# Batch 0's second half of outputs: transposed, as four units of seven block products, ahead of batch 1's folding

## The chip, the cores and the metric

The kernel runs on one core of a Trainium2 chip. The core has five engines with queues of their own: TensorE (PE, matrix products; PEld is its weight load), VectorE (DVE), ScalarE (ACT), GpSimd (POOL) and SyncE (SP, which here only issues DMAs). ACT and POOL issue DMAs too. Every engine works off its own queue in order and waits there for semaphores. The metric is device time in microseconds; the profile is one execution, taken by the hardware profiler.

## The reference

Two batches of 1024 tokens with 1024 features. After a layer norm, two linear maps are taken of the normed input, one with a block-masked weight and a bias (s), one with a dense weight plus a mixture of eight low-rank updates whose coefficients depend on the batch's mean token (y). The output is `x + s * silu(y)`.

```python
xn = _layernorm(x, axis=-1)
# s: blocks of 32x32 of the weight are dropped where the mask's block sum is 0
s = jnp.einsum('bsk,nk->bsn', xn, w_masked) + bias
# y: E = 8 updates of rank R = 64, mixed by coeffs of each batch
base = jnp.einsum('bsi,oi->bso', xn, W_org)
q = jnp.einsum('bi,ki->bk', xn.mean(axis=1), Wq)
coeffs = jax.nn.softmax(jnp.einsum('bk,ek->be', q, lora_keys) / math.sqrt(K), axis=-1)
h = jnp.einsum('bsi,eir->bser', xn, lora_down)
delta = jnp.einsum('be,bser,ero->bso', coeffs, h, lora_up)
g = _silu(base + delta)
x = x + s * g
```

All data are float32, and each product is made of three products of parts: a value is split into a high part (a copy into the type float32r, by ACT) and a low part (the difference, by DVE), and high x high, high x low and low x high are summed in PSUM. So a product of a 128x128 weight with 128x512 data costs three matmuls, and a contraction of 512 costs twelve, one *group*.

## The kernel before

**Folding.** The mixture is linear in the weights, so for each batch the kernel folds the low-rank part into the dense weight: W = W_org^T + down · (coeff · up). `scale_up` multiplies the 512 rows of `up` by the coefficients of the batch and splits them (four tiles `cut`). One *fold* (`y_prep`, `y_mul`, `y_sum`) makes 128 rows of 512 output columns of W: load a block of `down` (tile `ds`) and one of W_org (tile `wo`), split `ds` into `dhi` (ACT) and `dlo` (DVE), twelve matmuls into a PSUM tile `psw` (two of these), and an add on DVE of `psw` to `wo`. A half of the output (512 columns, `h`) takes eight folds (`kt`), a batch sixteen.

**Batch 0, plainly.** Tokens stand in PSUM's partitions: a `gemm` of one tile of 128 tokens and 512 output columns takes eight rows of the contraction, 24 matmuls. The order on PE is: a ramp with the first half (h = 0) of s; eight folds for y, h = 0 (L826); the phase y, h = 0, eight gemm tiles with the eight folds for h = 1 between them (`jobs_b`); the phase y, h = 1 (`jobs_c`), with the masking of the s weights of h = 1 beside it; then `s_tile`, the gemm tiles of s, h = 1, with batch 1's sixteen folds between them (L1075). The results of the first map of each pair stay in `stash`; `final_evac` multiplies, adds x and leaves the store to ACT (`store_late`).

**Batch 1, transposed, with seven products.** Here outputs stand in the partitions and tokens in the columns. A *unit* is a pair of blocks of 128 outputs for one of the maps (s or y), for all 1024 tokens: a 2x2 block product over halves of the contraction and halves of the tokens, done as seven block products instead of eight (Strassen's scheme in Winograd's form). `quad` (L1157) does a unit: seven groups of twelve matmuls, 84, into three PSUM tiles (`pa`, `pb`, `py`), with copies and adds between (`snap`, L1178, L1192, L1202, L1203). The seven sums of the data side are made once: `wide_load`, `wide_norm` (L911) and `wide_b` norm batch 1's transposed input and form differences, POOL stores them to DRAM (`xv`, `store_sums`), and `fill` loads and splits them into the tiles `xw`. The weight side is made for each unit one quad ahead: `unit_load` (s from the input `wu`, y from the folded weights `yu`, which the folds stored to DRAM from ACT), `unit_mask`, `unit_sum`, `unit_split`. There are eight units, and units 2k and 2k+1 share their outputs: the first writes `gate` tiles, the second multiplies, and `out_tile` adds x by a DMA that accumulates onto the SBUF tile (L1130, issued by POOL), after which SP stores the tile (L1134). The last unit loads x ahead instead (`res_load`).

**Means.** Batch 1's means and variances come from DVE (`bn_stats`, `nat_stats` L164), 16 instructions of 128x512.

**What sets the order.** On PE, DVE, ACT and POOL the program's own order holds (`manual_schedule`, L617); SP's order is chosen at build. Tiles come from pools with a fixed number of buffers; a tile that takes over a buffer waits until its last user is done, a DMA included. The pool `stage` has one tag `st` of six buffers of 128x512 which `ds`, `wo`, `us` and others share.

Of the kernel before, what the change touches and what calls it, by code (L numbers as in the profile page):

```python
# [32 lines left out]
def kernel(  # L33
# [25 lines left out]

    nc = tc.nc  # L60
# [31 lines left out]
    ones_r = c0pool.tile([P, P], F32R, name="ones_r")  # L92
    nc.vector.memset(ones_r.bitcast(F32), 1.0)
# [21 lines left out]
    keys_sb = c0pool.tile([P, E_], F32, name="keys_sb")  # L115
# [30 lines left out]
    def rstd_of(t):  # L146

        mv = small.tile([P, 2], F32, name="mv", bufs=10)
        nc.vector.bn_aggr(mv, stat[t])
        ve = small.tile([P, 1], F32, name="ve", bufs=3)  # L150
        nc.vector.tensor_scalar(ve, mv[:, 1:2], EPS, None, ALU.add)
        nc.gpsimd.tensor_tensor(rstd[:, t : t + 1], ve, mhalf, ALU.pow)
        means[t] = mv[:, 0:1]
# [10 lines left out]
    def nat_stats(b, i):  # L164
        t = b * TPB + i
        xn = nat_tile()
        nc.sync.dma_start(xn, x[t * P : (t + 1) * P, :])
        bn(t, xn, 0)
        bn(t, xn, 1)
        rstd_of(t)  # L170
# [87 lines left out]
    def mask_part(qr, c):  # L258
        mt = nat_tile(I32)
# [10 lines left out]
    def s_mul(dst, h, kt):  # L270
        st = stage.tile([P, NH], F32, name="ws", tag="st", bufs=6)
        nc.sync.dma_start(st, wT[kt * P : (kt + 1) * P, h * NH : (h + 1) * NH])
        v = st.rearrange("p (b i) -> p b i", i=32)
        nc.vector.tensor_tensor(
            v, v, m_sb[:, kt, 16 * h : 16 * (h + 1)].unsqueeze(2).to_broadcast([P, 16, 32]), ALU.mult
        )
        nc.scalar.copy(dst[:, kt, 0, :], st)  # L277
        staged[("s", h, kt)] = st

    def s_lo(dst, h, kt):  # L280
        st = staged.pop(("s", h, kt))
        nc.vector.tensor_tensor(dst[:, kt, 1, :], st, dst[:, kt, 0, :].bitcast(F32), ALU.subtract)


    csel = {}

    def coeffs(b):


        def sums():  # L290
# [3 lines left out]
            for h in range(2):  # L294
                ps = ps_s.tile([P, 4, P], F32, name="xrow", tag="ps_s")
# [14 lines left out]
        def query():  # L310
            qh = small.tile([P, 2], F32, name="qh")
            for h in range(2):
# [5 lines left out]
                else:  # L318
                    mp = csel[b][h]
                junk = stage_l.tile([P, NH], F32, name="junk", tag="g", bufs=2)  # L320
                nc.vector.scalar_tensor_tensor(
                    junk, mp, 1.0, wq_sb[:, h * NH : (h + 1) * NH], ALU.mult, ALU.mult, accum_out=qh[:, h : h + 1]
# [7 lines left out]
        def scores():  # L330
            sp = ps_s.tile([P, E_], F32, name="sp", tag="ps_s")
# [27 lines left out]
    def scale_up(b, h, homes=()):  # L359
        cu[(b, h)] = []  # L360
        for c in range(4):
            t = cupool.tile([P, 2, NH], F32R, name="cut", tag="cu")
            st = homes[c] if c < len(homes) else stage.tile([P, NH], F32, name="us", tag="st", bufs=6)
            nc.sync.dma_start(st, up[c * P : (c + 1) * P, h * NH : (h + 1) * NH])
# [8 lines left out]
    def y_prep(b, h, kt):  # L373
        ds = stage.tile([P, 4, P], F32, name="ds", tag="st", bufs=6)
        nc.sync.dma_start(ds, down[kt])
        ws = stage.tile([P, NH], F32, name="wo", tag="st", bufs=6)
        nc.sync.dma_start(ws, worgT[kt * P : (kt + 1) * P, h * NH : (h + 1) * NH])
        dhi = stage.tile([P, 4, P], F32R, name="dhi", bufs=2)
        dlo = stage.tile([P, 4, P], F32R, name="dlo", bufs=2)
# [21 lines left out]
    def y_add(dst, b, h, kt):  # L401
        y_sum(b, h, kt)
        y_hi(dst, b, h, kt)

# [4 lines left out]
    def y_fin(dst, b, h, kt):  # L409
        y_add(dst, b, h, kt)  # L410
        y_lo(dst, b, h, kt)
# [52 lines left out]
    def final_evac(kind, b, h, i, ps, res):  # L464
        t = b * TPB + i
        mine = stage_l.tile([P, NH], F32, name="mine", tag="g", bufs=2)
        if kind == "s":
            s_evac(mine, ps, b, i, h * NH, NH)
        else:
            y_evac(mine, ps, b, i)  # L470
        nc.vector.tensor_tensor(mine, mine, stash[(b, h, i)], ALU.mult)
# [815 lines left out]
```

## Time and profile before

| | us |
|---|---|
| three runs | 458.43, 462.94, 462.17; median 462.17 |
| the profiled execution | 462.08 |
| its span, first to last instruction | 460.1 |
| PE busy | 444.7 |
| DVE busy | 305.1 |
| ACT busy | 169.3 |
| POOL busy | 59.5 |
| bytes moved by DMA | 89.52 MB, 195 GB/s on average |

Stages by PE's work, in us from the start of the span: ramp and s, h = 0, of batch 0 to 70.6; folds for y, h = 0, to 92; the phase y, h = 0, with folds to about 160; the phase y, h = 1, to about 212; s, h = 1, with batch 1's folds to 305.7; eight quads, the last matmul ending at 455.2; the last adds and stores to the end.

A line of a group reads: line, engine, operation, tile written from tiles read, shapes, number of instructions | busy us, mean ns of one | idle time of the engine before them and what ended it. In a windows row the busy time and number of instructions of each engine follow the stretch's length, then the clock granted to PE (1.00 is full), the mean busy share of the 16 DMA engines, and GB/s. In a list of DMAs the last number is the median time from issue to landing. In a list of waits the three numbers are the total, the number of waits and the longest.

### The profile page before, as it was taken

The numbers are of one execution on the slowest core, as the hardware profiler recorded it, in microseconds if no ns is written. First come the engines' busy times: TensorE is split into PE (matmuls) and PEld (weight loads), VectorE is DVE, ScalarE is ACT, GpSimd is POOL, SyncE is SP. The second block draws the span as 40 slices with busy tenths as digits, with TensorE's granted clock in tenths as the row PEclk, the third lists the DMA queues.
The fourth block names the chain that finished last, engine by engine and source line by source line (L and its number), as shares of the span: only waits on it lengthen the run. The fifth ranks groups of instructions, "written<-read, shape, count | busy, mean of one in ns | idle before, by whom it ended". The sixth has DMA issues, their size and how long they took to land.

```text
span 460.1 us, 5752 instructions
## 1 busy us (share of the span) xinstructions
PE 444.7 (97%) x2047; PEld 365.4 (79%) x2047; DVE 305.1 (66%) x492; ACT 169.3 (37%) x277; POOL 59.5 (13%) x72
## 2 busy tenths in 40 slices
PE   7799999999999999997999999999999999999995
PEld 5689888888887888885888788877888888888884
DVE  5889778666775788866546776669466294465624
ACT  3576624363323132213324233158243422441510
POOL 3764210000010202230000000000020020002000
PEclk9899999999999999997999999999999999999999
DMA  8995406687862586799778985664274246218003
GB/s 267 390 350 196 146 24 205 183 281 255 287 230 93 186 317 227 277 309 303 243 249 276 297 274 152 207 219 137 79 147 134 85 98 177 91 24 220 31 1 114
DMA packets 47404, 89.52 MB, mean 195 GB/s; under 512 B 4752, under 2 KB 14992, under 8 KB 47376
## 3 DMA queue, kind: packets, MB, share of 16 engines
q1 hardware_dynamic: 32784, 70.28, 46.1%
q0 software_dynamic: 3840, 10.49, 8.9%
q10 hardware_dynamic: 10752, 8.39, 5.7%
q8 instruction: 16, 0.26, 0.2%
q14 instruction: 12, 0.10, 0.1%
HBM read 69.21 MB, written 19.92 MB: 194 GB/s over the span
## 4 chain that ended last, share of the span: by engine, by line
PE 85%; DVE 8%; DMA 4%; issue 1%; ACT 1%; SPq 0%; ACTq 0%; DVEq 0%
PE acc_ps L1147 23%; PE acc_ps L425 11%; PE acc_ps L426 11%; PE acc_ps L427 11%; PE py L1147 9%; PE psw L391 6%; PE psw L389 6%; PE psw L390 6%; DMA ws<-in_wT_dram 2%; DMA raw<-in_x_dram 1%; DVE slot L558 1%; DVE ramp L549 1%; DMA misc<-in_up_dram 1%; DVE st L144 1%; DVE xw L1002 1%
## 5 line engine op out<-in xcount | busy, mean ns | idle before, releaser
L1147 PE MATMUL acc_ps<-xw,ow 128*128 128x512 f32 x480 | 113.6, 393 | 0.4 <-ACT acc_ps L1178 0.4
L425 PE MATMUL acc_ps<-slot,xgrp 128*128 128x512 f32 (+1 forms) x288 | 107.4, 373 | 2.8 <-ACT slot L277 2.7
L426 PE MATMUL acc_ps<-slot,xgrp 128*128 128x512 f32 (+1 forms) x288 | 106.8, 371 | 2.7 <-DVE slot L558 2.7
L427 PE MATMUL acc_ps<-slot,xgrp 128*128 128x512 f32 (+1 forms) x288 | 106.4, 369 | 0.7 <-DVE xgrp L570 0.7
L1147 PEld LDWEIGHTS acc_ps<-xw,ow 128*128 128x128 f32 x480 | 90.0, 188 | 21.3 <-ACT acc_ps L1178 0.8
L426 PEld LDWEIGHTS acc_ps<-slot,xgrp 128*128 128x128 f32 x288 | 54.9, 191 | 12.6 <-DVE slot L558 3.6
L425 PEld LDWEIGHTS acc_ps<-slot,xgrp 128*128 128x128 f32 x288 | 54.8, 190 | 12.3 <-ACT slot L277 3.1
L427 PEld LDWEIGHTS acc_ps<-slot,xgrp 128*128 128x128 f32 x288 | 55.0, 191 | 10.2 <-DVE xgrp L570 1.1
L391 PE MATMUL psw<-cut,dlo 128*128 128x512 f32 x128 | 50.9, 397 | 0.8 <-DVE dlo L381 0.8
L389 PE MATMUL psw<-cut,dhi 128*128 128x512 f32 x128 | 51.0, 399 | 0.0
L390 PE MATMUL psw<-cut,dhi 128*128 128x512 f32 x128 | 50.6, 395 | 0.0
L1147 PE MATMUL py<-xw,ow 128*128 128x512 f32 x192 | 46.9, 392 | 0.0
L1147 PEld LDWEIGHTS py<-xw,ow 128*128 128x128 f32 x192 | 36.1, 188 | 8.1
L1047 DVE TENSOR_TENSOR ow<-raw,ow 128x1024 fp32r<-128x1024 f32 (+1 forms) x32 | 34.5, 1087 | 10.4 <-ACT ow L1046 10.4
L1130 POOL DMA_DIRECT2D gate<-in_xT_dram x12 | 10.5, 906 | 203.0 <-DVE gate L1128 133.9
L380 ACT CAST dhi<-ds 128x512 fp32r<-128x512 f32 x32 | 19.8, 617 | 40.0 <-PE psw L390 23.8
L396 DVE TENSOR_TENSOR wo<-wo,psw 128x512 f32<-128x512 f32 x32 | 22.0, 686 | 18.6 <-PE psw L391 18.5
L1046 ACT CAST ow<-raw 128x1024 fp32r<-128x1024 f32 (+1 forms) x32 | 29.4, 940 | 1.6 <-DVE wo L396 1.6
L391 PEld LDWEIGHTS psw<-cut,dlo 128*128 128x128 f32 x128 | 24.5, 192 | 6.7 <-DVE dlo L381 1.2
L390 PEld LDWEIGHTS psw<-cut,dhi 128*128 128x128 f32 x128 | 24.6, 192 | 5.4
L389 PEld LDWEIGHTS psw<-cut,dhi 128*128 128x128 f32 x128 | 24.6, 192 | 5.2
L1192 DVE TENSOR_TENSOR py<-py,s 128x512 f32<-128x512 f32 x8 | 5.6, 698 | 30.7 <-ACT s L1154 30.7
(160 smaller groups left out, 477.6 us busy)
## 6 DMA issues: line engine op xcount, KB each, us to landing
ds<-in_down_dram SPq DMA_DIRECT2D x32, 256.0 KB, 3.7
wo<-in_worgT_dram SPq DMA_DIRECT2D x32, 256.0 KB, 3.8
raw<-in_x_dram SPq DMA_DIRECT2D x11, 512.0 KB, 6.5
res<-in_x_dram SPq DMA_DIRECT2D x16, 256.0 KB, 3.8
out_dram<-res ACTq DMA_DIRECT2D x16, 256.0 KB, 2.7
raw<-in_wu_dram SPq DMA_DIRECT2D x8, 512.0 KB, 5.1
yu<-wo ACTq DMA_DIRECT2D x16, 256.0 KB, 4.1
xs<-xv SPq DMA_DIRECT2D x16, 256.0 KB, 4.0
```

The costliest lines, as they stand in the source:

```text
L380: nc.scalar.copy(dhi, ds)
L389: nc.tensor.matmul(ps, lhsT=dhi[:, c, :], rhs=u[c][:, 0, :], start=c == 0, stop=False)
L390: nc.tensor.matmul(ps, lhsT=dhi[:, c, :], rhs=u[c][:, 1, :], start=False, stop=False)
L391: nc.tensor.matmul(ps, lhsT=dlo[:, c, :], rhs=u[c][:, 0, :], start=False, stop=c == 3)
L396: nc.vector.tensor_tensor(ws, ws, ps, ALU.add)
L425: nc.tensor.matmul(ps, lhsT=xs[:, kt, 0, cols], rhs=w[:, kt, 0, wc], start=kt == 0, stop=False)
L426: nc.tensor.matmul(ps, lhsT=xs[:, kt, 0, cols], rhs=w[:, kt, 1, wc], start=False, stop=False)
L427: nc.tensor.matmul(ps, lhsT=xs[:, kt, 1, cols], rhs=w[:, kt, 0, wc], start=False, stop=kt == NKT - 1)
L1046: nc.scalar.copy(o[:, a:b, 0], raw[:, a:b])
L1047: nc.vector.tensor_tensor(o[:, a:b, 1], raw[:, a:b], o[:, a:b, 0].bitcast(F32), ALU.subtract)
L1130: nc.gpsimd.dma_start(g, xT[n * P : (n + 1) * P, S + t * NH : S + (t + 1) * NH], accum_op=ALU.add)
L1147: nc.tensor.matmul(ps, lhsT=o[:, a, wl, j, :], rhs=xw[j][:, m, xl, :], start=start and j == 0 and k == 0, stop=j == 3 and k == 2, skip_gro ...
```

## The change

*Units for batch 0.* The phases y, h = 1, and s, h = 1, of batch 0 are gone. Outputs 512 to 1023 of batch 0 are computed as batch 1's are: four units (s, y, y, s) of 84 matmuls, with the quad of before. Its results are stored transposed into the right half of the output's batch 0, and the host's `kernel()` reorders them. `upper_rows`, `upper_load`, `upper_a` and `upper_b` make the seven sums of the data side during the gemm phase of y, h = 0, from the tokens' split tiles that are there and the transposed input of the upper 512 tokens; three of the seven go to DRAM (`xv0`) and come back by `fill`.

*Order on PE.* Ramp and s, h = 0; eight folds for y, h = 0; eight gemm tiles of y, h = 0; eight folds of batch 0, h = 1; four quads of batch 0; sixteen folds of batch 1, first h = 1, then h = 0; eight quads of batch 1, the first with the weights of the fourth quad (`SAME`). Batch 1's wide sums and its coefficients are made during the first four quads (`extra`).

```diff
+        units = [(0, k, n) for k, n in zip("syys", (4, 4, 6, 6))]
+        units += [(1, k, n) for k, n in zip("syysysys", (6, 6, 0, 0, 2, 2, 4, 4))]
+        SAME = 4
...
+        for u in range(1, 4):
+            quad(u, unit_jobs(u + 1), extra[u])
...
+        for n, (h, kt) in enumerate(folds):
+            if n + 1 < len(folds):
+                y_prep(1, *folds[n + 1], n + 1 > 13)
+            store_folds()
+            y_mul(1, h, kt)
+            y_out(1, h, kt)
+            for m, j in take(2) if 1 <= n < 11 else ():
+                fill(xv1[j, :, XV1[m], :], m, j)
```

*Folds.* The folds stand alone, without gemm tiles between them. Of batch 0's eight for h = 1 six, and of batch 1's sixteen fourteen, load no `wo`: ACT copies the product to a tile `wy`, and a DMA that POOL issues adds W_org to it. The stores of the folded weights go from ACT's queue to POOL's, each issued ahead of the next fold's products; the tiles are 128x512, in four pieces of 128 columns.

```diff
+    def y_out(b, h, kt):
+        ps, ws = staged[(b, h, kt)]
+        if ws is None:
+            ws = staging("wy")
+            nc.scalar.copy(ws, ps)
+            nc.gpsimd.dma_start(ws, worgT[kt * P : (kt + 1) * P, h * NH : (h + 1) * NH], accum_op=ALU.add)
+        else:
+            nc.vector.tensor_tensor(ws, ws, ps, ALU.add)
+        del staged[(b, h, kt)]
+        n0 = 0 if b == 0 else 4 * h
+        fold_stores.append((
+            yu[b][n0 : n0 + 4, :, kt // 4, kt % 4, :].rearrange("m p n -> p m n"),
+            ws.rearrange("p (m n) -> p m n", n=P),
+        ))
...
+    def store_folds(keep=0):
+        while len(fold_stores) > keep:
+            nc.gpsimd.dma_start(*fold_stores.pop(0))
```

*Accumulating loads for means and for x.* Where a mean was subtracted by DVE, ACT now writes the negative mean into a tile and POOL issues a DMA that adds the input to it; the same for x in `final_evac`.

```diff
+        def upper_load(j):
+            t = cupool.tile([P, 2, NH], F32, name="uv", tag="cu")
+            nc.scalar.copy(t, upper[:, 0:1, :].to_broadcast([P, 2, NH]))
+            src = xT.rearrange("(h j p) n -> h j p n", h=2, p=P)[:, j, :, NH:S].rearrange("h p n -> p h n")
+            nc.gpsimd.dma_start(t, src, accum_op=ALU.add)
...
+        def wide_load(j, half):
+            t = pair("ac" if half == 0 else "bd")
+            wide[(j, half)] = t
+            kt = j + 4 * half
+            nc.scalar.copy(t, rows[:, 0])
+            nc.gpsimd.dma_start(t.rearrange("p g n -> p (g n)"), xT[kt * P : (kt + 1) * P, S : 2 * S], accum_op=ALU.add)
...
+        res = stash[(0, 0, i)]
+        nc.vector.tensor_tensor(res, res, mine, ALU.mult)
+        rows = slice(i * P, (i + 1) * P)
+        nc.gpsimd.dma_start(res, x[rows, 0:NH], accum_op=ALU.add)
+        late_stores.append((out[rows, 0:NH], res))
```

In all the program has 60 accumulating loads, where it had 12.

*Statistics of batch 1.* `nat_stats` makes two passes on ACT (a copy with a sum, a square with a sum) instead of `bn_stats` on DVE.

```diff
+        nc.scalar.activation(xn, xn, AF.Copy, accum_out=sm[:, 0:1])
+        neg = small.tile([P, 1], F32, name="neg1", bufs=TPB)
+        nc.vector.tensor_scalar(neg, sm[:, 0:1], -1.0 / D, None, ALU.mult)
+        nc.scalar.activation(xn, xn, AF.Square, bias=neg, accum_out=sm[:, 1:2])
```

*Unit weights.* `unit_load` takes 512 KB for one block of outputs (a pair of blocks is now neighbours, and `wu` is laid out so), and the split weights are held in five smaller tiles (`ow2`, `ow1`) instead of two whole sets. The last unit's last product is done in two halves of 256 columns.

*Rest.* The warm-up multiplies the tile `inv_s` instead of a tile of ones, which is gone. The tiles `st` of the folds of batch 1 are taken from the pool of the `gate` tiles, also six buffers.

## The prediction, made before the changed kernel ran

> **What bounds the kernel now.** I read the page first, then the chain by time, the stages by windows, the DMA landings, and the waits of the DMA queues. Page, busy time and chain:
>
> ```profile
> PE 444.7 (97%) x2047; PEld 365.4 (79%) x2047; DVE 305.1 (66%) x492; ACT 169.3 (37%) x277; POOL 59.5 (13%) x72
> PE 85%; DVE 8%; DMA 4%; issue 1%; ACT 1%; SPq 0%; ACTq 0%; DVEq 0%
> ```
>
> TensorE sets the time, so removed matmuls count in full, unless something else becomes late. The unit is a group of twelve 512-column matmuls (a fold, or one block product), from the chain by time:
>
> ```profile
> 333.72 2.72 PE py L1147 x12
> 364.23 8.16 PE acc_ps L1147 x36
> ```
>
> That is 2.73 us a group. Stages: the ramp and the first output half end at 70.6; from there to 305.7, where the quads begin, there are 80 groups (8 folds, 64 in gemms with 8 folds between, 64 more, 16 folds: 96+288+192+384 matmuls), 218.4 us of work in 235.1 us; the quads and the tail take 154.4 us. So 16.7 us are stalls, the largest around 210, where PE stood 2.73 us and came back at half clock:
>
> ```profile
> 212.78 0.80 PE L425 MATMUL acc_ps<-slot,xgrp 128*128 128x512 f32 x1 [2.73 <-ACT slot L277]
> 214.00:216.00 2.00, 2.00 (x6) 1.52 (x6) 1.64 (x4) 0.34 (x1) 0.00 (x0) 0.50 0.73 238
> ```
>
> The first line is the timeline, the second the windows (after the POOL count come clock, DMA share and GB/s). The half clock lasts from 212.8 to 218.8, matmuls 0.43 us apart: 14 matmuls cost 3.2 us more than at 0.227.
>
> The change rests on accumulating loads, and the kernel has twelve, of exactly the shape used by the new ones (256 KB, 128 rows of 2 KB). DMA list, landing times, the SP queue's waits, and two rows of the timeline:
>
> ```profile
> gate<-in_xT_dram POOLq DMA_DIRECT2D x12, 256.0 KB, 6.1
> ds<-in_down_dram SPq DMA_DIRECT2D x32, 256.0 KB, 3.7
> yu<-wo ACTq DMA_DIRECT2D x16, 256.0 KB, 4.1
> raw<-yu SPq DMA_DIRECT2D x8, 512.0 KB, 3.8
> DMA to landing us min/median/max: 4.6/6.1/8.6
> SPq L1134 <- DMA gate<-in_xT_dram: 35.0, 12, 4.9
> 333.32 0.97 POOL L1130 DMA_DIRECT2D gate<-in_xT_dram  x1 [128.24 <-DVE gate L1128]
> 339.15 4.04 SPq L1134 DMA_DIRECT2D out_dram<-gate  x2
> L487 POOL DMA_DIRECT2D xv<-tt x8 | 4.4, 552 | 0.4 <-issue 0.4
> ```
>
> An accumulating load takes 4.6 to 8.6 us until its data may be used, against 3.7 for a plain one, and a store that needs it holds its whole queue: SP stood 35.0 us in twelve such waits. The first was issued at 333.32, its store at 339.15, 5.83 us later. A plain store costs POOL 0.55 us to issue.
>
> **The change, part by part.** *Matmuls.* Removed: sixteen gemm tiles of 24 (the y half interleaved with s, 384 matmuls). Added: four units of 84 (336). That is 48 fewer, four groups, 10.9 us. With no stall left anywhere, the sum is 70.6 + 76 groups × 2.73 (8 folds, 16 in gemms, 8 folds, 28 in units, 16 folds) = 207.5, + 154.4 for eight quads and tail. The last product in two column halves shortens the tail by two DVE steps of 128x512 (0.75 and 0.69) that become 128x256 (0.42 each, the row of L439), 0.6 us. 70.6 + 207.5 + 154.4 − 0.6 = 431.9 us of span: 28.2 us below 460.1.
>
> *The fold stages.* Before, every fold's sum was a DVE add of 0.69 us into a loaded tile, and batch 1's sixteen were stored from ACT. Now 6 of batch 0's 8 folds and 14 of batch 1's 16 do this: ACT copies the product (0.6), POOL issues the accumulating load of W_org, and the fold's store is POOL's next instruction. It waits for the landing. The next fold's accumulating load stands behind it in POOL. So each such fold takes POOL a period P = L + s, L the landing, s the issue of the store. L: 4.6 to 5.8 where nothing was queued before it, 6.4 to 8.6 behind other accumulating loads; here a store goes out just ahead of each, between the two; I take the median, 6.1. s: 0.55 for 128 pieces; the new store has 512 of 512 bytes, so up to four times that, 2.2; as ACT's issue of that same pattern took 0.37 us against SP's 0.33 for a plain one, I take 0.55. P = 6.65 us, against 2.73 of PE. Buffers let PE run about four folds ahead (six staging tiles that loads of `down` share, two PSUM banks); the rest is paced by POOL.
>
> Batch 1, from T, the end of the fourth quad (who waits for whom is read from the built program, the times from the rows). SP holds the third fold's `down` load behind the output store that waits for an accumulating load issued at T−0.6: issue T+5.6, landing T+9.5, its cast on ACT 0.6, behind which stands the second fold's copy, 0.6: accumulating load 1 (counting from 0) at T+10.8, load 9 at T+10.8+8P. The last fold's `down` load reuses the tile of store 9: landing L, store 4.3 (the 4.1 of the row and what xv's took, 4.3), load 3.8, cast 0.6, matmuls 2.73. End T+22.2+8P+L against T+43.7, so 8P+L−21.5 late. PE stands several us before it, so a half clock as at 212 adds 3.2: 8P+L−18.3 = 53.2+6.1−18.3 = 41.0 us. What comes next is not late: the following quad reuses weights, and the last stores land before the second quad needs them.
>
> Batch 0, from T0, the end of the last gemm tile: first accumulating load at T0+3.6, load 5 at +5P, its store +L, two more stores 1.1, landing 4.3, the 512 KB loads of the second unit 4.2, then sum 0.7, cast 1.05, copy 0.57 on ACT (the copy that the first quad's last product needs stands behind that cast). That product starts at T0+15.5+5P+L = T0+54.9 instead of T0+21.8+16.4 = T0+38.2: 16.7 us. The other way, by the last fold's `down` load behind store 2, gives 15.0+2P+L−21.8+3.2 = 15.8; the larger counts.
>
> *What hides, and what not.* Batch 1's statistics go from DVE (16 × 0.68) to ACT (two passes of 1.05 + 0.19 a tile, 19.8 us); with 8 evacuations, casts and copies ACT has some 35 us of work in the gemm stage of 43.7 us. But ACT also issues the output stores, and each now waits for an accumulating load (6.1 us after its issue, one tile of 5.46 us later): ACT falls behind by up to 0.5 us a tile, DVE too has about 43 us of work there. The four PSUM banks hide most of that. Cost 0 to 6, I take 3. In the first four quads batch 1's wide loads bring DVE 2 × 1.22 + 4 × 0.69 = 5.2 us a quad on 9 to 13 of 19.2, which fits; but ACT's copy into a pair tile waits for that tile's store (4.3 after DVE's last subtraction) and holds the snapshots that PE's third product needs. Cost 0 to 12, I take 6. The warm-up on another constant of ones' shape, the bigger counts of DMA (89 to 101 MB, the busiest slices moved 390 GB/s, the mean is 195) and the coefficients in the fourth quad cost nothing by themselves: DVE has gaps there (13.8 us idle before its weight masks, L1032).
>
> Sum: 431.9 + 41.0 + 16.7 + 3 + 6 = 498.6 of span. The profiled execution had 462.08 against its span 460.1, so 2.0 beside it: 500.6 us; the median of three is 462.17, the same, so nothing is shifted.
>
> A rule speaks for the change instead. The Trainium skill, "DMA: Bandwidth & Descriptors", section "Anatomy of one DMA — SWDGE (gpsimd) path", fits a transfer from that queue as 2.0 us plus the bytes at 436 GB/s: 2.6 us for 256 KB. By that estimate P is 3.15 us, batch 0 loses nothing, batch 1 9.5, and the time is about 452 us, faster. The rows say 4.6 at the least for the accumulating form, so the measurement decides.
>
> **Rivals.** (1) *Faster*: POOL's pairs do not pace the folds. Deciding point: the two stage terms are 13P+2L−41.0; with L = P−0.55 that is 15P−42.1, and with the 9 us of the small terms it meets the 28.2 us of gain at P = 4.1 us. Below 2.73 nothing is lost: 431.9+9+2 = 443 us. For it: the POOL trace has no DMA that waits for a DMA, so the wait itself is not seen there. Against it: SP's twelve waits, and that the shortest landing alone exceeds 4.1. (2) *No change*: P near 4.1, about 462. (3) *Much slower*: in the busy stretch 198 to 201, at DMA share near 1.0, xv's stores took 7.2 to 10.3 us to land; if the fold stage is such a stretch, L = 9.2, P = 9.75, 13P+2L−41.0 = 104, 547 us. Against it: per period 1.28 MB moves, 190 GB/s at P = 6.65, about the mean. (4) The change does not save what it says: the built program has 60 fewer 512-column matmuls and 24 more of 256 columns, which is the 48; no chance.
>
> **How the numbers follow.** The POOL period as forecast 0.80, much slower 0.10, no change 0.03, faster 0.07. Low end: L = 4.6, P = 5.15, small terms zero: 431.9+35.2+2 = 469. High end: L = 7.2 (the median of the eight later loads), s = 1.1: 81.3, so 431.9+81.3+2+9 = 524, and 4 more from the small terms' upper ends: 528. What lies outside is the rest of rivals 1 to 3. One per cent, 4.6 us, is about what can be told from no change. Faster 0.07, within 0.03, slower 0.90.
>
> **What would show it.** In the changed profile: POOL's waits headed by the fold's store waiting for the DMA wy<-in_worgT_dram, with about 20 waits of some 5 us; accumulating loads 6 to 7 us apart; PE busy about half of the batch 1 fold stage, which lasts some 84 us instead of 44, with the granted clock near 0.5 in parts; the chain through DMA and POOL there. The four units at 77 us of products, the first some 5 us longer. It is wrong if POOL shows accumulating loads less than 4 us apart, if the landing row is below 4 us, or if the lost time lies in the units instead.

## The result, and the profile after

The changed kernel takes 561.44 us, the median of four runs (559.51 to 561.90), against 462.56 for the kernel before (four runs, 458.43 to 463.53): a ratio of 1.215, 95% interval 1.207 to 1.223. It is slower, as forecast, but by 99 us instead of 38, and 33 us beyond the upper end of the range. The profiled execution took 561.35 us, its span 559.6.

The page of the changed kernel: busy time, the granted clock in 40 slices of 14 us, what the DMA engines moved, and the shares of the chain of waits.

```profile
PE 463.3 (83%) x2019; PEld 371.4 (66%) x2019; DVE 302.8 (54%) x483; ACT 232.3 (42%) x380; POOL 127.0 (23%) x152
PEclk9999999778987979988877988887999999999999
DMA packets 44590, 101.59 MB, mean 182 GB/s; under 512 B 5264, under 2 KB 7568, under 8 KB 44560
PE 28%; DMA 14%; issue 12%; ACT 3%; DVE 3%; POOL 2%; SPq 0%; POOLq 0%; ACTq 0%; DVEq 0%
```

TensorE was 97% busy before and 85% of the chain; now it is 83% busy and 28% of the chain, and DMA and "issue" together hold nearly as much of the chain as it does. There are fewer matmuls (2019 instead of 2047), but PE's busy time has grown by 18.6 us. The clock row says why: it is below 9 in sixteen of the slices from the eighth to the 28th.

The changed kernel by stages: the columns are the busy times of PE, PEld, DVE, ACT and POOL with their counts, then clock, DMA share and GB/s. The six stretches are batch 0's gemm stage, its second fold stage, the first unit quad, the second to fourth, batch 1's sixteen folds, and batch 1's eight quads with the tail.

```profile
91.58:155.70 64.12, 48.36 (x209) 38.72 (x207) 36.63 (x65) 33.84 (x58) 17.60 (x23) 0.87 0.80 222
155.70:197.90 42.20, 28.10 (x97) 19.38 (x98) 24.23 (x34) 18.40 (x31) 11.44 (x14) 0.88 0.80 215
197.90:225.10 27.20, 23.59 (x102) 19.56 (x101) 7.81 (x10) 10.90 (x16) 4.60 (x6) 0.87 0.53 126
225.10:318.50 93.40, 68.99 (x263) 54.62 (x262) 48.61 (x79) 28.86 (x42) 23.71 (x34) 0.85 0.69 194
318.50:399.80 81.30, 55.88 (x194) 40.84 (x193) 29.22 (x45) 29.00 (x52) 20.63 (x25) 0.85 0.83 225
399.80:559.60 159.80, 153.39 (x685) 126.42 (x683) 84.48 (x109) 58.74 (x89) 16.18 (x19) 1.00 0.42 118
```

At 2.73 us a group, the products of the first five stretches need 43.7, 21.8, 19.1, 57.4 and 43.7 us: 185.7 of the 308.2 they take. So 122.5 us are lost between 91.6 and 399.8. PE stands for 83.3 us of them (308.2 less 224.9 busy); the other 39.2 are busy time beyond the products. By the trace's records PE was busy for 57.4 us of that stretch while the clock stood at half, which costs 28.7; the rest are small matmuls (masks, transposes) and the slower first matmul behind each wait. The eight quads behind it took no longer than before: from their first matmul to their last they take 155.7 us, as in the other kernel (299.55 to 455.2).

Two of the places. First the gemm stage, from the timeline (start, length, what ended the idle time before, in brackets):

```profile
94.95 1.39 POOL L880 DMA_DIRECT2D uv<-in_xT_dram  x1 [0.46 <-ACT uv L878]
105.98 0.69 DVE L860 TENSOR_TENSOR uv<-uv 128x512 f32<-128x512 f32 x1 [10.13 <-DMA uv<-in_xT_dram]
106.22 1.25 POOL L880 DMA_DIRECT2D uv<-in_xT_dram  x1 [9.88 <-issue]
113.97 0.38 PE L257 MATMUL mp<-r,misc 128*128 128x8 bf16 x8 [11.34 <-DVE r L247]
```

DVE stands 10.1 us for the first accumulating wide load; POOL issues the second only when the first has landed, 11.3 us after it; and eight tiny mask matmuls, which wait for a DVE step behind all this, stand in PE's own order between two gemm tiles. Free PSUM banks do not help there. Behind the gap the gemm's matmuls came 0.43 us apart, at half clock.

Second, batch 1's fold stage: POOL's timeline, and from the views of waits what POOL waited for over the whole run, and what SP, PE and ACT waited for in that stage (total us, times, longest):

```profile
333.43 0.87 POOL L438 DMA_DIRECT2D wy<-in_worgT_dram  x1 [0.49 <-ACT wy L437]
338.76 0.78 POOL L430 DMA_DIRECT2D yu<-wy  x1 [4.45 <-DMA wy<-in_worgT_dram]
339.52 0.89 POOL L438 DMA_DIRECT2D wy<-in_worgT_dram  x1
346.68 0.80 POOL L430 DMA_DIRECT2D yu<-wy  x1 [6.27 <-DMA s<-xv]
347.46 0.90 POOL L438 DMA_DIRECT2D wy<-in_worgT_dram  x1
```

```profile
POOL yu L430 <- DMA wy<-in_worgT_dram: 81.2, 18, 6.3
```

```profile
SPq L1021 <- DVE xgrp L857: 17.7, 6, 6.1
SPq L1021 <- DVE slot L857: 12.7, 9, 3.0
PE psw L405 <- ACT dhi L396: 17.9, 6, 5.9
PE psw L405 <- ACT cut L381: 5.1, 1, 5.1
ACT dhi L396 <- DMA ds<-in_down_dram: 25.9, 9, 7.3
```

The pairs are as forecast: a store that waits, then the next accumulating load, 6.1 and 7.9 us apart here. But SP, too, stands 30 us in that stage, with refills of operands (L1021) that wait for their staging tile, and the next load of `down` is queued behind each pair of refills. PE's own waits end there: of its 25.4 idle us 17.9 are for ACT's cast of `down` (`dhi`), which waits for that load, 5.1 for the scaled rows of `up` (`cut`) of the second half, and 2.2 for a low part.

### The profile page after: what moved, and what is told of

It is laid out like the page before. It is cut to its first block, busy times and chain, and to the rows that moved or that the text cites. A ratio compares the mean times of both kernels' runs of the same rounds, so it can differ in the third digit from the quotient of the medians.

```text
span 559.6 us, 5879 instructions
## 1 busy us (share of the span) xinstructions
PE 463.3 (83%) x2019; PEld 371.4 (66%) x2019; DVE 302.8 (54%) x483; ACT 232.3 (42%) x380; POOL 127.0 (23%) x152
## 3 DMA queue, kind: packets, MB, share of 16 engines
q1 hardware_dynamic: 29328, 63.46, 32.8%
q0 software_dynamic: 14080, 35.66, 29.4%
## 4 chain that ended last, share of the span: by engine, by line
PE 28%; DMA 14%; issue 12%; ACT 3%; DVE 3%; POOL 2%; SPq 0%; POOLq 0%; ACTq 0%; DVEq 0%
PE acc_ps L1107 19%; PE py L1107 6%; DMA ds<-in_down_dram 4%; DMA bd<-in_xT_dram 3%; DMA rest<-xv 2%; DMA gate<-in_xT_dram 1%; PE psw L405 1%; PE psw L406 1%; DMA ac<-in_xT_dram 1%; PE psw L407 1%; DMA raw<-in_wu_dram 1%; DMA yt<-xv 1%; POOL gate L1089 1%; DVE xgrp L857 1%; ACT xgrp L856 1%
## 5 line engine op out<-in xcount | busy, mean ns | idle before, releaser
L1107 PE MATMUL acc_ps<-slot,ow 128*128 128x512 f32 (+1 forms) x444 | 111.9, 404 | 18.9 <-ACT acc_ps L1150 15.4
L1107 PEld LDWEIGHTS acc_ps<-slot,ow 128*128 128x128 f32 x444 | 86.4, 199 | 39.4 <-ACT acc_ps L1150 17.4
L1107 PE MATMUL acc_ps<-xgrp,ow 128*128 128x512 f32 x288 | 71.3, 398 | 0.0
L1107 PEld LDWEIGHTS acc_ps<-xgrp,ow 128*128 128x128 f32 x288 | 55.5, 193 | 11.8
L461 PE MATMUL acc_ps<-slot,xgrp 128*128 128x512 f32 (+1 forms) x160 | 57.3, 358 | 2.7 <-DVE slot L569 2.7
L460 PE MATMUL acc_ps<-slot,xgrp 128*128 128x512 f32 (+1 forms) x160 | 58.1, 363 | 0.1
L462 PE MATMUL acc_ps<-slot,xgrp 128*128 128x512 f32 (+1 forms) x160 | 57.0, 357 | 0.7 <-DVE xgrp L581 0.7
L397 DVE TENSOR_TENSOR dlo<-ds,dhi 128x512 fp32r<-128x512 f32 x32 | 21.9, 687 | 37.1 <-ACT dhi L396 37.1
L405 PEld LDWEIGHTS psw<-cut,dhi 128*128 128x128 f32 x96 | 20.1, 209 | 29.7 <-ACT dhi L396 20.5
L430 POOL DMA_DIRECT2D yu<-wy x20 | 15.9, 794 | 93.0 <-DMA wy<-in_worgT_dram 81.2
L396 ACT CAST dhi<-ds 128x512 fp32r<-128x512 f32 x32 | 19.6, 616 | 40.9 <-DMA ds<-in_down_dram 28.6
L1107 PE MATMUL py<-slot,ow 128*128 128x512 f32 x144 | 36.5, 405 | 0.0
L461 PEld LDWEIGHTS acc_ps<-slot,xgrp 128*128 128x128 f32 x160 | 31.1, 195 | 7.4 <-DVE slot L569 3.6
L462 PEld LDWEIGHTS acc_ps<-slot,xgrp 128*128 128x128 f32 x160 | 31.1, 194 | 5.5 <-DVE xgrp L581 1.1
L1107 PE MATMUL py<-xgrp,ow 128*128 128x512 f32 x144 | 34.6, 389 | 0.0
```

The lines of the kernel that those rows point to most:

```text
L396: nc.scalar.copy(dhi, ds)
L397: nc.vector.tensor_tensor(dlo, ds, dhi.bitcast(F32), ALU.subtract)
L405: nc.tensor.matmul(ps, lhsT=dhi[:, c, :], rhs=u[c][:, 0, :], start=c == 0, stop=False)
L460: nc.tensor.matmul(ps, lhsT=xs[:, kt, 0, cols], rhs=w[:, kt, 0, wc], start=kt == 0, stop=False)
L461: nc.tensor.matmul(ps, lhsT=xs[:, kt, 0, cols], rhs=w[:, kt, 1, wc], start=False, stop=False)
L462: nc.tensor.matmul(ps, lhsT=xs[:, kt, 1, cols], rhs=w[:, kt, 0, wc], start=False, stop=kt == NKT - 1)
```

## The experiments

Each is one profiled execution beside one of the kernel before (459.57 to 461.60). Stages that an edit does not touch differ by up to 6 us between runs, as what comes ahead of them shifts; a difference below that is not read as an effect. The table has the time, and the stages as the traces give them: C is the gemm stage, D the time from its last matmul to the first quad, Q the four quads, F batch 1's folds.

| run | us | C | D | Q | F |
|---|---|---|---|---|---|
| products alone | | 43.7 | 21.8 | 76.5 | 43.7 |
| changed kernel | 561.4 | 64.1 | 42.2 | 120.6 | 81.3 |
| e1_keep | 562.6 | 65.0 | 44.6 | 115.3 | 84.5 |
| e2_wo | 558.3 | 65.1 | 44.3 | 116.2 | 78.5 |
| e3_mask | 563.3 | 53.7 | 53.2 | 120.8 | 82.0 |
| e4_wide | 558.0 | 64.8 | 43.2 | 113.3 | 82.0 |
| e5_uv | 552.6 | 58.4 | 40.9 | 119.3 | 81.1 |
| e6_store | 559.5 | 64.8 | 45.0 | 114.7 | 81.6 |
| e7_quarter | 545.1 | 64.8 | 40.7 | 106.3 | 77.3 |
| e8_ds | 561.6 | 63.8 | 40.6 | 123.9 | 78.3 |
| e9_all | 538.3 | 44.5 | 53.7 | 108.8 | 79.1 |
| e10_rows | 531.3 | 44.5 | 52.1 | 109.5 | 72.1 |
| e11_fp | 545.8 | 44.5 | 56.7 | 107.8 | 79.7 |
| e12_late | 550.6 | 44.4 | 61.7 | 108.1 | 79.2 |
| e13_quads | 552.1 | 44.5 | 60.7 | 112.4 | 77.3 |
| e14_q | 510.9 | 44.4 | 50.6 | 100.5 | 63.1 |
| e15_split | 534.1 | 44.4 | 53.9 | 109.0 | 72.3 |
| e16_qsplit | 513.4 | 44.4 | 50.2 | 100.6 | 63.7 |
| e17_stats | 524.7 | 44.2 | 43.0 | 107.7 | 73.5 |
| e18_nores | 527.0 | 44.5 | 50.0 | 108.1 | 72.7 |

### One part undone at a time

**e1_keep** lets one store stay behind in both fold loops:

```diff
-            store_folds()
+            store_folds(1)
             y_mul(1, h, kt)
```

> The stores of the folds go out one fold later on POOL, so that the next accumulating load no longer stands behind the store that waits for the last one; the loads themselves stay. Theory (order on POOL paces the folds, a period is one landing plus one issue): two loads are under way at once, the period of 6.4 us falls to about 3.4, the loss of 37.7 us in batch 1's fold stage to 10 to 18, batch 0's second fold stage gains some 5 to 10: 525 to 535 us. Rival (the accumulating transfers share one limit, so two at once take twice as long): the period stays near 6 us, the landing grows to 10 or more, 555 to 565 us.

562.6 us, and the fold stage no shorter (84.5). The first theory, which was the prediction's own, falls: the stores' waits for the loads did go, and nothing came of it. The view of POOL's waits in that stage now begins

```profile
POOL wy L438 <- issue: 16.7, 5, 4.4
POOL yu L430 <- issue: 14.3, 10, 4.1
```

so POOL stands for something that no semaphore shows. The landings of the accumulating loads were 5.0 us in the median, not 10: the rival's mechanism is not seen either, though its time is.

**e2_wo** loads W_org plainly:

```diff
-                y_prep(1, *folds[n + 1], n + 1 > 13)
+                y_prep(1, *folds[n + 1])
```

and the same in batch 0.

> The twenty accumulating loads of W_org become plain loads by SP, one fold ahead, and a DVE add of 0.69 us; the stores stay on POOL. Theory (the accumulating form and its wait are the cost): batch 1's fold stage falls from 81.4 to 44 to 52 us and batch 0's by 5 to 12, 510 to 525 us. Rival (the stage is bound by its bytes at DMA share 0.83, and by the stores of 512 pieces): the plain loads move the same bytes, the stage stays above 65 us, 540 us or more.

558.3 us, F 78.5: taking the accumulating form out of the fold stage gains nothing there beyond the spread, as long as the rest is there.

**e3_mask** takes the mask matmuls out of the way:

```diff
             mask_spread(qr)
-            mask_apply_mm(qr)
-            mask_apply_cp(qr)
...
-                5: [J(scale_up, 0, 1)],
+                5: [J(f, q) for q in (2, 3) for f in (mask_apply_mm, mask_apply_cp)] + [J(scale_up, 0, 1)],
```

> The two groups of mask matmuls and their copies go from the second and fourth gemm tile of batch 0's y half to behind the sixth. Theory (PE stood 15.7 us because these matmuls, in its own order between gemm tiles, waited for a DVE that waited for an accumulating load, and the half clock that follows costs some 4 more): the gemm stage falls from 64.1 to 46 to 50 us, total 543 to 549. Rival (DVE and ACT are late all the same, and PE waits for them at the evacuations or at the next stage): less than 6 us of it come through, 555 us or more.

563.3 us. The gemm stage did lose 10 us, but PE stood as long at the next one, as its first fold in the timeline shows:

```profile
156.32 0.80 PE L403 MATMUL psw<-cut,dhi 128*128 128x512 f32 x1 [10.25 <-ACT dhi L394]
```

The rival holds: C and D together are 106.9 us, 106.3 before the edit. PE's place in the order only decided where DVE's and ACT's lag was paid.

**e4_wide** makes batch 1's wide loads plain:

```diff
-            nc.scalar.copy(t, rows[:, 0])
-            nc.gpsimd.dma_start(t.rearrange("p g n -> p (g n)"), xT[kt * P : (kt + 1) * P, S : 2 * S], accum_op=ALU.add)
+            nc.sync.dma_start(t.rearrange("p g n -> p (g n)"), xT[kt * P : (kt + 1) * P, S : 2 * S])
...
+            nc.vector.tensor_tensor(t, t, rows[:, 0], ALU.add)
```

> Batch 1's wide loads become plain loads by SP, and the means are added by DVE (1.2 us each, eight of them). Theory (the 36 us lost in the second to fourth quad come from the accumulating form: ACT's copies into the pair tiles and its waits, and the 8.5 us of landing): 20 to 30 us come back, 531 to 541 us. Rival (three pair tiles for eight loads, and the DVE work, are the limit whatever the form): the loads wait for the same stores, now on SP ahead of the weight loads, and less than 10 us come back, 551 us or more.

558.0 us; the quads got 7.3 us shorter, a little over what untouched stages vary by. Less than 10 us came back, as the rival says.

**e8_ds** issues the loads of `down` ahead of the refills (on top of e1_keep):

```diff
+            if n + 2 < len(folds):
+                ds_load(1, *folds[n + 2])
```

> As e1_keep, with each load of down issued one fold earlier on SP, ahead of the refills that it stood behind. Theory of chains: PE's waits for ACT's cast of down (some 25 us in batch 1's fold stage) go, 535 to 545 us. Theory of bytes: the same traffic in another order, within 4 us of e1_keep, 558 to 566.

561.6 us. F is 6 us below e1_keep's, no more than the spread, Q 8.6 above it (what lengthened the quads there was not found). PE's waits for the cast of `down` fell only from 18.8 to 13.7 us: SP now stands 19 us with loads of `down` whose tile a late store still holds, the next chain in line.

**e5_uv** makes batch 0's wide loads plain, by SP, and adds the mean on DVE:

```diff
-            nc.scalar.copy(t, upper[:, 0:1, :].to_broadcast([P, 2, NH]))
-            nc.gpsimd.dma_start(t, src, accum_op=ALU.add)
+            nc.sync.dma_start(t, src)
...
+            nc.vector.tensor_tensor(t, t, upper[:, 0:1, :].to_broadcast([P, 2, NH]), ALU.add)
```

> The changed kernel with only batch 0's four wide loads made plain, by SP, and their mean added by DVE (1.2 us each). Theory (in batch 0's gemm stage DVE stood 10.1 us for the first of them, and POOL 9.9 us before it could issue the second): the stage falls from 64.1 to 46 to 52 us; if the next stage doesn't take it back, 545 to 549 us, and 555 to 561 if it does, as in e3_mask. Rival (the mask matmuls are late by the mask loads and ACT's sums): the stage stays above 58.

552.6 us, between the two totals of the theory. C is 58.4, not 46 to 52: the mask matmuls still hold PE for 9.8 us, now behind DVE's own work on the wide sums. But C and D together lose 7.0 us, and D did not take it back. Of the single parts it is the only one that clearly paid.

### The bytes

**e6_store** (on top of e1_keep) and **e7_quarter** (on the changed kernel) keep the order of the work and cut transfers to 32 of 128 rows, so that a fold's store has 128 pieces instead of 512; e7 for instance

```diff
-            nc.sync.dma_start(st, src)
+            nc.sync.dma_start(st[0:32], src[0:32])
```

> As e1_keep, with each store of a fold, and each load that reads them back, cut to a quarter of its rows (the outputs of the y units are computed from parts that are not filled). No instruction moves, and no fold waits for these stores but through a staging tile three folds later; what falls away is 4.7 MB of store traffic on POOL's queue and 4.7 MB of reads, most of these after 400 us. Theory of bytes (the stretch from 92 to 400 us is bound by what the 16 DMA engines can move, their share being 0.83 in batch 1's fold stage): at 74 engine-us per MB on POOL's queue (29.4% of 16 engines' span for 35.66 MB) the stage gets 10 to 16 us shorter, total 540 to 550. Theory of chains (folds are paced by SP's order: refills that wait for a tile, ahead of the loads of down): less than 4 us, 557 or more.

> A quarter of the rows in the stores and reads of the folds' sums, in the stores of both batches' wide sums, and in the refills of operands (outputs are then computed from unfilled parts); order, waits and engine work as in the changed kernel, but for ten small memsets. 25 MB fall away of 101.6. Theory of bytes: some 20 of these MB lie between 92 and 400 us, at 46 to 74 engine-us per MB they are worth 58 to 92 us: 470 to 505 us. Theory of chains: only the landings get shorter, by 1 to 2 us each: 525 to 545 us.

559.5 and 545.1 us. The theory of bytes falls as stated: in e7_quarter, with a third less traffic there (12.6 MB instead of 18.3), the fold stage is only 4 us shorter, within the spread, the gemm stage not at all. But the quads gave back 14 us, where five stores of wide sums a quad go out; there the transfers count, though bytes and landings were cut together.

e6_store shows one thing more: with one store kept behind and with small stores, POOL's longest wait in the fold stage is for ACT's copies of the products, and no "issue" is left. The stage still takes 81.6 us, so neither of POOL's orders paces it in the changed kernel:

```profile
POOL wy L438 <- ACT wy L437: 40.5, 11, 7.3
```

### All accumulating loads gone, then POOL's stores

**e9_all** is e2, e3, e4 and e5 together.

> e2_wo, e3_mask and e4_wide together, and batch 0's wide loads plain by SP with the mean added by DVE: no accumulating load is left between 92 and 400 us but the eight of batch 0's outputs and those of the units. Theory of bytes: the bytes stay, but the 13.6 MB change from the dearer form (74 engine-us per MB on POOL's queue) to 46, 24 us of all 16 engines: 535 to 545. Theory of chains on accumulating loads that cover for one another: 490 to 520. If neither holds (the single gains of 3 us add up), 550 to 558.

538.3 us: 23 us, where e2 to e5 one by one gave 3, −2, 3 and 9. C is at its products' time; D takes more than half of that gain back. F is still 79.1. Its timeline, POOL's stores beside SP's loads of W_org, showed what e1's "issue" was:

```profile
333.28 0.33 SPq L391 DMA_DIRECT2D wo<-in_worgT_dram  x1
333.57 0.75 POOL L428 DMA_DIRECT2D yu<-wo  x1 [4.22 <-issue]
```

SP's load takes the tile that the store before has released by landing, and 0.29 us after it POOL's next store begins. No dependence of the program links that store to the one before it; by the trace's landings 19 of the 24 such stores begin 0.30 to 0.36 us after the one before has landed.

**e10_rows** stores 128 rows of 2 KB instead of 512 pieces of 512 bytes:

```diff
-            yu[b][n0 : n0 + 4, :, kt // 4, kt % 4, :].rearrange("m p n -> p m n"),
-            ws.rearrange("p (m n) -> p m n", n=P),
+            yu[0][kt] if b == 0 else yu[1][h, kt], ws
```

> As e9_all, but each fold's sum is stored as 128 rows of 2 KB instead of 512 pieces of 512 bytes (the unit's load then gathers the pieces, by SP). In the trace of e9_all every store of POOL begins 0.3 us after the landing of the one before, 4 to 6 us apart, with its sum long there. Theory (a transfer of 512 pieces keeps POOL from issuing the next until it has landed; staging tiles come free late and SP stands with the loads of W_org): batch 1's fold stage falls from 79 to 55 to 65 us, batch 0's by 3 to 8: 510 to 522 us. Rival (SP's refills, waiting for a tile, or the bytes pace the folds): 533 us or more.

531.3 us, F 72.1. The waits went as the theory says; POOL's waits over the whole run held "yu L428 <- issue: 48.1, 11, 6.2" in e9_all, and now the stores wait for their own sums:

```profile
POOL yu L428 <- DVE wo L438: 89.8, 23, 9.1
```

The size was 7 us, not 14 to 24, between the two theories. It is the fastest of the kernels that compute everything, and still 70 us behind the kernel before.

**e11_fp, e12_late, e13_quads** go on from there, one edit each: refills by POOL (`nc.gpsimd.dma_start(st, src)`), output stores three tiles late (`store_late(3)`), the third and fourth wide sums two products later.

> As e10_rows, with the refills of operands issued by POOL instead of SP, so that a refill that waits for its tile no longer stands ahead of the loads of down and W_org. Theory (that order is a second chain of nearly the same length): batch 1's fold stage falls to 48 to 55 us, 5 to 25 us below e10_rows, more if the stores were not the limit there. Rival (bytes: DMA share 0.83 in that stage): less than 4 us below e10_rows.

> As e11_fp, with the stores of batch 0's first outputs three tiles behind their accumulating load on ACT instead of one. Theory (ACT stood 1.2, 3.9, 4.1 and 4.2 us for these landings in e9_all, ahead of the casts of down that the folds wait for): batch 0's second fold stage gets 8 to 14 us shorter. Rival (its folds wait for the loads of down behind the weight loads): less than 3 us.

> As e12_late, with batch 1's third and fourth wide sums two products later after their loads, and the coefficients one product later. Theory (in the second to fourth quad, DVE stood 6.5 us at a time for a wide load, with the weight sums and splits that PE needs queued behind): the four quads fall from 109 us by 8 to 14 us. Rival (the waits come from the weight loads and output stores on SP): less than 3 us, or longer by the coefficients that come later.

545.8, 550.6 and 552.1 us: all three theories fall. Refills on POOL stand behind the stores, which wait 45.8 us for their sums there (F 79.7); with the later stores D is 5 us longer, not shorter; with the later sums the quads are 4 us longer, not shorter.

### Bytes again, with the orders out of the way

**e14_q** is e10_rows with the quarter rows of e7; **e15_split** is e10_rows with

```diff
+            while loaded:
+                split(*loaded.pop(0))
             for m, j in take(2) if 1 <= n < 11 else ():
-                fill(xv1[j, :, XV1[m], :], m, j)
+                fill(xv1[j, :, XV1[m], :], m, j, loaded)
```

where `fill` only notes the split; **e16_qsplit** is both.

> As e10_rows, with a quarter of the rows in the folds' stores and reads, the wide sums' stores and the refills, as in e7_quarter (outputs are then computed from unfilled parts). In the changed kernel this cut gained 16 us in all and 4 in batch 1's fold stage. Theory (once POOL's two orders are gone, bytes are the limit: e10_rows moves 19.9 MB there at a DMA share of 0.86): some 7.7 MB less, the fold stage falls from 72 to 50 to 58 us, the four quads from 109 to 95 to 100: 485 to 505 us. Rival (waits in the order of ACT and SP still pace it, whatever the bytes): fold stage 68 or more, total 518 or more.

> As e10_rows, with each refill's cast and subtraction in batch 1's fold stage one fold after its load. In e10_rows ACT stood some 25 us there for refills that had not landed, with the next casts of down queued behind. Theory of orders: the fold stage falls from 72 to 60 to 66 us, 519 to 525 us. Theory of bytes: the same traffic, 70 us or more, 528 or more.

> e14_q and e15_split together. If bytes and orders each hold a part, the fold stage comes near its 43.7 us of products: 46 to 52 us, and the total is 478 to 498. If something else holds it (DVE's 37 us, the granted clock of 0.88), it stays above 58.

510.9, 534.1 and 513.4 us. Windows of the fold stage in e10_rows and in e14_q (the last three columns are clock, DMA share and GB/s):

```profile
298.40:370.70 72.30, 54.54 (x194) 39.94 (x193) 37.36 (x60) 22.46 (x39) 9.41 (x17) 0.88 0.86 276
```

```profile
287.20:350.40 63.20, 50.35 (x194) 38.29 (x193) 38.70 (x62) 22.32 (x39) 8.69 (x17) 0.92 0.72 207
```

The cut that was worth 4 us in this stage with POOL's orders and the accumulating loads in place is worth 9 without them, and another 9 in the quads. Splitting later is worth nothing. 63 us is neither theory's number: of the 19.4 us above the products 6.7 are busy time (50.35 against 43.7), 4.3 of it half clock, and the rest idle time that no run took away: 6.0 us for casts of `down`, 4.1 for the second half's `cut`, 2.2 for a low part.

### What D brings from the gemm stage

**e17_stats** returns from `nat_stats` for the last four tiles, **e18_nores** leaves out the accumulating load of `final_evac`; both on e10_rows.

> As e10_rows, without the statistics of the last four tiles of batch 1 (their loads, ACT's two passes of 1.05 us, DVE's small steps; the values of the first four stand in for them, so batch 1's outputs are of another scale). Theory (PE stood 11 us at the start of batch 0's second fold stage because ACT and DVE came 10 us late out of the gemm stage, and these passes, each with two turns between ACT and DVE, are why): the wait falls below 4 us, total 520 to 525 us. Rival (ACT is held by the output stores that wait for their accumulating load): the wait stays above 8, 528 or more.

> As e10_rows, without the accumulating load of x into batch 0's first outputs, which are stored without it. Theory of e17_stats: ACT no longer stands for the landings, but its statistics stay: PE's wait of 11 us stays above 6, total 524 to 529 us. Rival (the landings hold ACT): the wait falls below 4, the second fold stage from 41 to under 32 us, 515 to 521 us.

524.7 and 527.0 us. The first fold of D in the timelines of e17_stats and e18_nores:

```profile
143.21 0.50 PE L407 MATMUL psw<-cut,dhi 128*128 128x512 f32 x1 [4.70 <-ACT dhi L398]
```

```profile
146.13 0.79 PE L403 MATMUL psw<-cut,dhi 128*128 128x512 f32 x1 [10.12 <-ACT dhi L394]
```

In e10_rows the wait was 11.38 us. Half the statistics take 6.7 us of it away and 9 off D; the landings, 1.3 and 2, which is within the spread. In e10_rows the statistics on ACT are the larger part, as the theory said, though the wait stayed above the 4 us that it gave.

## Why the prediction was wrong

The direction was right, and so were the count of matmuls and the ramp. The size was not: of the 127.7 us between 431.9 without stalls and 559.6, it had 66.7. The steps that failed most are the two small terms for what hides: they counted the engines' work and not their waits in order, 9 us where 56.4 were lost. By its terms:

- **Batch 1's fold stage**: forecast 41.0, measured 37.6. The pairs are there, 81.2 us of POOL's waits in 18 (about 20 were expected), some 6.3 us a period (333.43 to 384.19 over eight) against 6.65; the issue of a store was 0.79 us, not 0.55, the landing 5.4, not 6.1. But "the rest is paced by POOL" failed: e1_keep took that order away, e6_store the waits for many pieces as well, and the stage stayed at 84.5 and 81.6. PE stood for loads of `down` on SP, and 5.1 us for the second half's `cut`, which no term of the sum has. Other paces of nearly the same length lay there: POOL's stores of 512 pieces were worth 7 us (e10_rows) and the bytes 9 (e14_q) only once others were gone; SP's order of refills and `down` is seen in the waits, but no run that changed it gained more than the spread. The number was right by luck. PE was 69% busy there, not about half.
- **D and the first quad**: forecast 16.7, measured 28.5 (20.4 and 8.1). The step that failed is the start: it took ACT and DVE to be ready when the last gemm tile ended ("first accumulating load at T0+3.6"). It came at T0+10.7; ACT had stood 6.8 us for a landing of x, ahead of a cast of `down`:

```profile
163.04 0.62 ACT L396 CAST dhi<-ds 128x512 fp32r<-128x512 f32 x1 [6.76 <-DMA stash<-in_x_dram]
166.37 0.85 POOL L438 DMA_DIRECT2D wy<-in_worgT_dram  x1
```

  The place was wrong as well: PE did not wait at the first quad's last product but in D itself, 8.6 us for casts of `down` and 5.4 for their low parts, and 3.6 us at the first quad's small transposes. In e10_rows ACT's statistics are the larger part of such a lag (e17_stats); that they are in the changed kernel is not shown, as no run took them, or the landings, out of it.
- **The gemm stage**: forecast 3, measured 20.4. "The four PSUM banks hide most of that" failed: the step counted engine work (35 and 43 us, which fit) and not waits, and it didn't price the wide loads by the new 11.3 us between two of them. Spare banks help only the evacuations; the mask matmuls wait in PE's own order for DVE. Yet the mask order was not the cause but the place (e3_mask); with plain wide loads C and D lost 7.0 us less (e5_uv).
- **Second to fourth quad**: forecast 6, measured 36.0, the largest miss. The 5.2 us of DVE work did fit; what was left out is that DVE stood 23.8 us for the wide loads and kept the weight sums behind, for which ACT stood 22.4 us. Accumulating loads are worth at most some 7 us of it (e4_wide), smaller transfers 9 to 14 (e14_q, e7_quarter). Batch 1's eight quads, the same code without the wide sums, took no longer than before, so it is the wide work, and the coefficients with it, that costs. Some 24 us of the stage (100.5 against 76.5, the first quad included) are not explained: the one attempt at their order (e13_quads) went the other way.
- **Batch 1's quads**: forecast 0, and they took no longer than before. The 6.0 us that the stretch takes over the sum's 153.8 are mostly the sum's own: it lets the quads of the kernel before begin at 305.7, but their first two groups ran ahead of that, so 431.9 is two groups, 5.5 us, short, and the 16.7 us of stalls before are 11.2:

```profile
299.55 0.63 PE L1147 MATMUL acc_ps<-xw,ow 128*128 128x512 f32 x2
```
- **Cost at nothing**: that the bigger counts of DMA and the coefficients in the fourth quad "cost nothing by themselves" was wrong. The transfers cut in e7_quarter are worth 16 us in the changed kernel and 20 once the accumulating loads and the 512 pieces are gone. No mean tells that: from 91.6 to 399.8 the DMA share is 0.53 to 0.83, and in the kernel before it was 0.73 to 0.74 from 70.6 to 305.7, where PE hardly stood. And PE stood 4.8 us for the coefficients' matmul:

```profile
PE sp L333 <- DVE qb L325: 4.8, 1, 4.8
```
- **The clock**: one half clock of 3.2 us was priced in the fold stage's term, one in D's other way. There were fifteen gaps of 2.6 us and more, and with them 28.7 us lost to slow matmuls: nearly half of the 61.0 that the sum lacked.
- **The range**: the upper ends that it gives for its two small terms, 6 and 12, add 9 us to its 524 and not 4; it would have ended at 533, still 28 us short.

So what the prediction's own last list named came true on both sides: POOL's waits in the folds look as it said, and more of the lost time than forecast lay in the units. Rival 3, much slower, gave 547 by a longer landing; the time is nearer to that number, but the landing was shorter, not longer.

What stays open: the 24 us in the quads, 13 of the 19 us above the products in e14_q's fold stage, and some 22 us in C and D of e17_stats (87.2 against 65.5).

## What to carry to other kernels

When several chains of nearly one length pace a stage, pricing one of them can give about the right time, and undoing it still gives nothing; look at what the busiest engine itself waits for, ask what is second before you expect a gain, and test by taking several away together. Work moved beside TensorE is not judged by whether its busy time fits: every transfer that an engine waits for in order holds what is queued behind it, and a matmul in TensorE's own queue that waits for such an engine is not covered by spare banks. Count the gaps, too: each one that halves the clock is paid a second time, some 1.9 us here.

## What the runs showed of the hardware that was not expected

*POOL's transfers of many pieces go one at a time.* Of the accumulating wide loads with 256 pieces of 2 KB, the second was issued 11.3 us after the first, with 9.9 us idle that no wait of the program explains; stores of 512 pieces began 0.3 us after the one before had landed. Transfers of 128 pieces did not show this one at a time (five stores of 128 rows went out 0.55 us apart, and e6_store, e10_rows); but with three to five of them under way POOL stood for "issue" too (2.86 us at 235.80, 4.85 at 264.74), until 0.31 us after an earlier one had landed. So it looks like a limit on the pieces under way. The Trainium skill, "DMA: Bandwidth & Descriptors", section "SWDGE vs HWDGE vs iDMA", says that GpSimd writes the descriptors of its transfers into rings that lie in a reserved part of SBUF. A ring too small for two such transfers would explain it; this kernel reserves 1024 bytes for it, and no run changed that, so it is not shown.

*The length of a gap alone does not tell whether the clock falls.* In the windows behind each gap of the changed kernel the clock was 0.50 to 0.58 after all fifteen gaps of 2.6 us and more, and 1.00 after gaps of 2.24, 1.81, 1.59 and 0.95 us. But in e5_uv it fell behind a gap of 1.50 us, and in e16_qsplit it did not behind one of 3.41 us. Here the windows behind the gaps of 2.63 and 2.24 us, and behind those two:

```profile
295.70:299.00 3.30, 3.30 (x9) 2.59 (x10) 2.41 (x4) 0.00 (x0) 1.05 (x2) 0.56 0.36 139
321.40:325.00 3.60, 3.60 (x16) 2.95 (x17) 0.53 (x1) 0.59 (x1) 0.63 (x1) 1.00 1.09 269
163.20:166.60 3.40, 3.40 (x9) 2.64 (x8) 0.69 (x1) 1.10 (x2) 0.00 (x0) 0.50 0.92 244
252.80:256.00 3.20, 3.18 (x14) 2.63 (x15) 2.69 (x4) 1.83 (x3) 0.25 (x1) 1.00 0.85 201
```

By the records of the twenty traces, from 90 us to the last matmul, every stretch at half clock lasts 3.41 us or a whole multiple of it. In the 3.41 us ahead of each of the 227 falls PE was busy for at most 56%; in all 1926 such windows that left the clock full it was busy for at least 45%. So what counts is how much of such a window PE stands idle, about half of it; the gap of 3.41 us lay half in each of two. The Trainium skill, "TensorE: Matmul & The Clock Gate", Part 1, puts it at one idle window of about 3.4 us and says that the window runs on its own, whatever the kernel does. The windows agree with the runs, but they need not be wholly idle. In the changed kernel a gap that halved the clock cost 1.9 us on the average on top of itself (28.7 over fifteen).

*Accumulating loads took more of the DMA engines' time.* POOL's queue took 29.4% of the 16 engines' span for 35.66 MB, 74 engine-us per MB, SP's 32.8% for 63.46 MB, 46. With the twenty loads of W_org moved from one to the other (e2_wo), the first fell by 557 engine-us and the second grew by 358.
